# Causal attention with FFN on one core: masked quarters of the diagonal score blocks left out, short rows flipped, planner offsets split by token tile

## The chip, the cores and the metric

The kernel runs on one core of a Trainium2 chip. The metric is the device time of one execution in microseconds (us), lower is better.

## The reference, cut to what matters

The input is x of shape (8, 1024, 256): 8 batches of 1,024 tokens with 256 channels. All arithmetic is float32. There are 16 heads of width 64.

```
h   = layernorm(x)
q,k,v = h @ Wq, h @ Wk, h @ Wv                      # per head, 256 -> 64
s   = q k^T / 8 + rel_table[clip(j - i + 16, 0, 32)]   # bias by distance
s   = -inf where j > i                              # causal
a   = softmax(s) v ; o = concat(a) @ Wp + bp
x   = x + layernorm(o)
y   = layernorm(x); y' = y shifted by one token
r   = sigmoid((mu_r y + (1-mu_r) y') @ W_r)
f   = r * (relu((mu_k y + (1-mu_k) y') @ W_k)^2 @ W_v)
out = x + layernorm(f)
```

Only keys at or before the query count, so of each 128x128 block of scores on the diagonal the upper right triangle is masked. One quarter of that block, 64 queries by 64 keys, is masked in full.

## The kernel before

**Tiling.** The work is cut into 64 units, one for each batch and pair of heads. A unit's 1,024 queries are eight token tiles `tb` of 128 rows. Tile `tb` needs keys 0 to n = (tb + 1) x 128. Tiles 4 to 7 are "long" (n over 512): their scores are made in two parts of n/2 columns, each in one of two long PSUM tiles (`sl`, two banks each, both heads beside each other). Tiles 0 to 3 are "short": one part, with each head's scores in one of four single PSUM banks (`pm`). A unit is worked through in four steps, each with one long and one short tile: `STEPS = ((7, 1), (6, 0), (5, 3), (4, 2))`.

**Score matmuls (line 1000).** `part` in `do_scores` issues four matmuls: two output halves of 64 queries (`o` = 0 and 64, PSUM partitions 0 to 63 and 64 to 127) times two heads (64 rows of the array each). They use the array as four 64x64 tiles. All other matmuls contract over 128 rows and are issued in pairs of 64 output columns by the helper `matmul` (line 392), or likewise in `do_av` (line 1252), so the array is two 128x64 tiles there. The planner calls the two uses modes "rows" and "cols".

**Softmax.** For a part that reaches the diagonal, VectorE adds the bias with the mask from the table `bm` to the last 144 columns (`bias`, line 1029), then takes the negated row maximum (`top`, line 1037). ScalarE computes exp with the sum (line 1057). VectorE takes reciprocals (line 1124), GpSimd scales the rows (line 1145). The weights `p` are then transposed in 32x32 blocks by VectorE into `blocks` (line 1166), and 16 DMAs for each half unit (`shuffle`, line 1226) move the blocks into `d`, which `do_av` multiplies with v. Its result goes to `oT` (128 channels by 256 tokens), the stationary operand of `project_out`.

**Order.** Nothing is issued as it is written. `Planner.add` collects tasks, each with an engine, an assumed cost, buffers and a priority. `Planner.run` simulates the engines from these costs, and the instructions are then issued in the order of the best plan. A task's first priority is its step plus an offset from the table `RANK`, found by `kind(eng, fn)`, an engine and function name. `URGENT` is what a switch between the modes "rows" and "cols" costs in the choice of the next matmul task. Each engine carries out its queue in order, SP's DMA queue too.

**Start.** A prologue loads weights, builds one row of the bias table (`line`), writes it to DRAM as `skew`, and reads it back as `bm` with a row step that shifts each row by one column. Behind `bm` come the loads of `wp_sb` and of three raw FFN weights.

Of the kernel before, what the change touches and what calls it, by code (L numbers as in the profile page):

```python
# [8 lines left out]
F32 = mybir.dt.float32  # L9
# [30 lines left out]
SWITCH = 0.09  # L40
ISSUE = 0.66
STEP = 9.0
URGENT = 1.05


RANK = {
    "pe:part.go": -0.82,
    "dve:top.go": 1.9,
    "act:exp.go": -3.14,
    "dve:bias.go": 1.02,  # L50
    "pool:do_scores.behind": 6.53,
    "act:do_scores.<lambda>": -2.87,
    "pool:do_scores.both": 6.86,
    "dve:do_scores.<lambda>": -0.11,
    "pool:do_scores.<lambda>": -4.38,
    "pool:scale.go": 6.48,
    "dve:one.go": 1.8,
    "pe:do_qk.go": -0.33,
    "act:do_qk.<lambda>": -20.88,
    "sp:shuffle.move": 21.5,  # L60
    "pe:do_v.go": 0.57,
    "act:do_v.<lambda>": 11.6,
    "sp:load_wqk.go": -9.79,
    "sp:load_wv.go": 1.65,
    "pe:do_av.go": 0.22,
    "act:save.<lambda>": -6.41,
    "sp:load_rows.<lambda>": -6.4,
    "dve:norm_stats.go": 2.38,
    "pe:one.go": -0.19,
    "dve:one.plus_old": -14.51,  # L70
    "pool:normed.power": -0.11,
    "pool:normed.go": 6.49,
    "dve:by_dma.<lambda>": -1.51,
    "sp:by_dma.leave": -24.02,
    "sp:by_dma.<lambda>": -17.77,
    "act:by_dma.place": 4.69,
    "pool:plus.go": -26.3,
    "pool:s2.<lambda>": -47.14,
    "act:s3.go": 2.12,
    "dve:s4.go": 3.56,  # L80
    "pe:s5.go": 0.53,
    "act:s5.<lambda>": 17.56,
    "pool:s5.<lambda>": -0.97,
    "pe:second.go": -2.43,
    "act:s6.<lambda>": 22.56,
    "dve:s7.<lambda>": -5.69,
    "sp:s9.<lambda>": -14.9,
    "pe:some.go": 1.42,
    "act:normed.go_edge": -15,
}  # L90


def kind(eng, fn):
    return eng + ":" + ".".join(x for x in fn.__qualname__.split(".")[-3:] if x != "<locals>")


class Buf:
# [10 lines left out]
class Ring:  # L108


    def __init__(self, pool, shape, tag, n):
        self.pool, self.shape, self.tag, self.n, self.owners = pool, shape, tag, n, []

    def __call__(self, name, view=None):
        return Buf(self, name, view)
# [2 lines left out]
class Task:  # L118


    def __init__(self, eng, cost, fn, prio, mode, banks, mb):
        self.eng, self.cost, self.fn, self.prio, self.mode = eng, cost, fn, prio, mode
        self.banks, self.held, self.readers, self.mb = banks, (), [0] * banks, mb
        self.deps, self.after, self.makes, self.frees = [], [], [], []
        self.users, self.behind, self.left, self.first, self.seen = [], [], 0, 0.0, None


class Planner:
# [5 lines left out]
    ENGINES = ("pe", "sp", "act", "dve", "pool")  # L134

    def __init__(self, banks):
        self.tasks, self.gate = [], None
        self.free = dict.fromkeys(self.ENGINES, 0.0)
        self.mode, self.moved = None, 0.0
        self.bank_free = dict.fromkeys(range(banks), 0.0)  # L140

    def add(
# [12 lines left out]
    ):  # L155


        t = Task(eng, cost, fn, prio, mode, banks, mb)
        t.deps = list(deps)
        if self.gate is not None:  # L160
            t.deps.append(self.gate)
# [116 lines left out]
    def run(self, rounds, urgent=1.0, rank={}):  # L278

        new, self.tasks = self.tasks, []  # L280
        for t in new:
            deps = {}
            for d in t.deps:
                deps.update(dict.fromkeys(d if isinstance(d, list) else [d]))
            deps.pop(t, None)
            for d in deps:
                if d.seen is None:
                    d.users.append(t)
                    t.left += 1
                else:  # L290
                    t.first = max(t.first, d.seen)
            for d in dict.fromkeys(t.after):
                if d is not t and d not in deps and d.seen is None:
                    d.behind.append(t)
                    t.left += 1
        best, prio = None, {t: (t.prio + rank.get(kind(t.eng, t.fn), 0.0)) * STEP for t in new}
        for _ in range(rounds):
            plan = self.simulate(new, prio, urgent)
            if best is None or plan[0][-1][2] < best[0][-1][2]:
                best = plan  # L300
            prio = self.late(*plan[:2])
        order, held, state = best
        self.free, self.bank_free, self.mode, self.moved = state
        for t, _, _, seen in order:
            t.held = held.get(t, ())
            for b in t.makes:
                b.tile = b.ring.pool.tile(
                    b.ring.shape, F32, tag=b.ring.tag, name=b.name, bufs=b.ring.n
                )
                if b.view is not None:  # L310
                    b.tile = b.view(b.tile)
            t.fn()
            t.seen = seen
# [3 lines left out]
def tile_attn_ffn_block(  # L317
# [57 lines left out]
    acts = ctx.enter_context(tc.tile_pool(name="acts", bufs=1))  # L375

    bank = [ps_m.tile([P, HB], F32, name=f"pm{i}") for i in range(4)]
    plan = Planner(len(bank))
    add = plan.add

    def pm(t, i=0):

        return bank[t.held[i]]
# [4 lines left out]
    def matmul(dst, lhs, rhs, first, last):  # L388
# [18 lines left out]
        "ynT": Ring(acts, [P, NC, CT + 1], "ynT", 1),  # L407
        "q": Ring(acts, [P, T], "q", 2),
        "k": Ring(acts, [P, T], "k", 2),
        "v": Ring(acts, [P, NT, P], "v", 1),  # L410
        "sl": Ring(ps_l, [P, 2, HB], "sl", 2),
        ("p", "long"): Ring(acts, [P, T], "pl", 3),
        ("p", "short"): Ring(acts, [P, HB], "ph", 4),
        "carry": Ring(small, [P, NC], "carry", 2),
# [30 lines left out]
    def load_wqk(u, prio):  # L445

        pr = units[u][1]
        for name, w in (("q", Wq), ("k", Wk)):
# [9 lines left out]
                    )  # L458

            add("sp", 2 * ISSUE, go, w=[buf], prio=prio)  # L460

    def load_wv(u, prio):
        pr = units[u][1]
# [187 lines left out]
    def project_out(b, c, prs, prio):  # L651
# [6 lines left out]
        def one(k):  # L658
            def go():
                for pr in prs:  # L660
                    matmul(
                        pm(t)[:, :C],
                        oT[b, pr, c].tile[:, (1 - k) * P : (2 - k) * P],
                        wp_sb[:, pr, :],
                        (pr == prs[0]),
                        (pr == prs[-1]),
                    )

            t = add(
                "pe",  # L670
# [303 lines left out]
    def do_scores(u, tb, prio):  # L974


        n = (tb + 1) * P
        size = "long" if n > HB else "short"
        parts = [(0, n // 2), (n // 2, n)] if n > HB else [(0, n)]
        pr = units[u][1]  # L980
        q, k = qkv[u, "q"], qkv[u, "k"]
# [5 lines left out]
        def part(i, c0, c1):  # L987

            sl = R["sl"](f"s_{what}_{i}") if size == "long" else None
            keep = [sl] if sl else []  # L990

            def s(hh):
                return sl.tile[:, hh, : c1 - c0] if sl else pm(t, hh)[:, : c1 - c0]

            def go():
                for half in range(2):
                    for hh in range(2):
                        rows = slice(hh * D, (hh + 1) * D)
                        o = half * D
                        nc.tensor.matmul(  # L1000
                            s(hh)[o : o + D],
                            q.tile[rows, tb * P + o : tb * P + o + D],
                            k.tile[rows, c0:c1],
                            start=True,
                            stop=True,
                        )

            t = add(
                "pe",
                0.05 + (c1 - c0) * 0.00169,  # L1010
                go,
                r=[(q, tb // 4)] + [(k, g) for g in range((c1 - 1) // HB + 1)],
                w=keep,
# [8 lines left out]
            def bias(h0, h1):  # L1022
                def go():
# [1 line left out]
                        dst = sl.tile[:, :, c1 - c0 - w : c1 - c0]  # L1025
                        src = bm[:, 2 * pr : 2 * pr + 2, BW - w :]
                    else:
                        dst, src = s(h0)[:, n - w : n], bm[:, 2 * pr + h0, BW - w :]
                    nc.vector.tensor_tensor(dst, dst, src, ALU.add)  # L1029

                cost = 0.07 + (h1 - h0) * w / 960
                done = add("dve", cost, go, t, bm_done, r=keep, prio=prio - 0.5)
                ready.update({hh: done for hh in range(h0, h1)})

            def top(h0, h1):
# [115 lines left out]

        for hh in range(2):
            scale(hh)
        return z

    def turn(z, prio):

# [6 lines left out]
        def one(hh, p):  # L1164
# [9 lines left out]
                add("dve", 0.065 + n / 960, go, *state["move"], r=[p], prio=prio)  # L1174
            )

        for hh in range(2):
            one(hh, z["p"][hh])

    def turn_by_pe(z, g, prio):  # L1180

# [119 lines left out]
    with tc.tile_pool(name="prep", bufs=1) as prep:  # L1301
# [36 lines left out]
            prio=-4,  # L1338
        )
        bm_done = add("sp", ISSUE, lambda: nc.sync.dma_start(bm, moved), skew_done, prio=-4)  # L1340
        load_wv(0, -3)
        wp_done = add(
            "sp",
# [16 lines left out]
        for g in range(2):  # L1360
            do_qk(0, "k", g, -2)
            do_qk(0, "q", g, -2)
        load_wqk(1, -1)
        for half in range(2):
            soft[0, half] = do_scores(0, STEPS[0][half], -1)
        add(
# [62 lines left out]
    for m in range(LAST):  # L1429
# [3 lines left out]
            for half in range(2):  # L1433
                soft[m + 1, half] = do_scores(nu, STEPS[nst][half], m)
        if st == 0:
            do_av(u - 1, 0, m)
        if st == 2:
            do_av(u - 1, 1, m)
            do_v(u, 0, m + 0.3)
        if st == 3:  # L1440
            if u + 2 < NU:
                load_wqk(u + 2, m)
            do_v(u, 1, m + 0.3)
            if u + 1 < NU:
                load_wv(u + 1, m)
        if m + 1 < LAST:
# [7 lines left out]
            else:  # L1454
                turn(soft.pop((m, half)), m)
        if st % 2 and (u < NU - 1 or st == 1):
            shuffle(u, st // 2, m)
        if st == 0:
            do_qk(u + 1, "k", 0, m + 0.4)
            do_qk(u + 1, "k", 1, m + 0.6)  # L1460
        elif st == 1:
            do_qk(u + 1, "q", 1, m + 0.4)
        elif st == 2:
            do_qk(u + 1, "q", 0, m + 0.4)
    b = B - 1
    for g in range(2):
        do_av(NU - 1, g, LAST)
# [46 lines left out]
```

## Time and profile before

| | |
|---|---|
| time, median of 3 runs | 2208.03 us (2206.36 to 2208.11) |
| the profiled execution's own time | 2206.46 us |
| its span, first to last instruction | 2204.7 us, granted TensorE clock 0.997 |
| TensorE (PE) busy | 2172.5 us (99%) |
| VectorE (DVE) busy | 1967.5 us (89%) |
| GpSimd (POOL), ScalarE (ACT) busy | 1524.2 us (69%), 1412.6 us (64%) |
| DMA | 388.92 MB in 272,596 packets; the main queue holds 72.1% of 16 engines |

"Busy" is the time in which the engine has at least one instruction under way. The chain of work that ended last gives 92% of the span to PE. PE matmuls are pipelined and their ends are modelled, so it is best to read starts: the time from one group's start to the next group's start.

### The profile page before, as it was taken

The page shows a single profiled execution, that of the slowest core. Times are in us where ns is not written, and L with a number is a line of the kernel's source. Part 1 is how long each engine was busy: PE and PEld are TensorE (multiplying, and loading weights), DVE is VectorE, ACT ScalarE, POOL GpSimd, SP SyncE. Part 2 cuts the span into 40 slices and gives each one's busy share as a digit, 9 for nine tenths or more (in the row PEclk, how much of TensorE's full clock was granted, in tenths as well). Part 3 has the DMA queues.
Part 4 walks back from the last instruction along what each step waited for, and adds up shares of the span by engine and source line. Part 5 has one row for each costly group of instructions (what it writes and reads, how often), then busy time and mean ns, then how long its engine had stood idle before and what let it go on. Part 6 is the DMA issues. An engine that isn't in the chain of part 4 may idle for free.

```text
span 2204.7 us, 61232 instructions
## 1 busy us (share of the span) xinstructions
PE 2172.5 (99%) x21312; PEld 1175.2 (53%) x21312; DVE 1967.5 (89%) x4460; ACT 1412.6 (64%) x4314; POOL 1524.2 (69%) x3709
## 2 busy tenths in 40 slices
PE   7999999999999999999999999999999999999997
PEld 3455555555555545555555555555555555555565
DVE  5989999989999899998999889999898989999876
ACT  5666766657576676766667566666666656666554
POOL 4666677766777667776677757776677866677553
PEclk9999999999999999999999999999999999999999
DMA  5878877778777887777877787777777768777560
GB/s 159 188 179 204 197 176 173 173 192 194 184 168 174 195 192 173 173 172 194 190 177 173 168 205 191 176 173 170 196 186 174 180 167 214 180 183 180 128 160 25
DMA packets 272596, 388.92 MB, mean 176 GB/s; under 512 B 142624, under 2 KB 199968, under 8 KB 272160
## 3 DMA queue, kind: packets, MB, share of 16 engines
q1 hardware_dynamic: 272144, 384.87, 72.1%
q8 instruction: 170, 2.79, 0.5%
q14 instruction: 138, 1.13, 0.2%
q10 hardware_dynamic: 144, 0.14, 0.0%
HBM read 59.91 MB, written 25.29 MB: 39 GB/s over the span
## 4 chain that ended last, share of the span: by engine, by line
PE 92%; DVE 4%; DMA 1%; POOL 1%; ACT 1%; issue 0%; SPq 0%; ACTq 0%; DVEq 0%; POOLq 0%
PE pm L392 47%; PE pm L1252 22%; PE s L1000 16%; PE pm L1000 7%; DVE nmax L1037 1%; DVE blocks L1166 1%; DMA out_dram<-r 1%; DMA skew<-line 0%; DMA raw<-in_L_ffn_W_r_dram 0%; POOL p L1145 0%; ACT p L1057 0%; DVE pm L1029 0%; DVE xk L801 0%; DVE s L1029 0%; DMA tab<-in_L_attn_rel_table_dram 0%
## 5 line engine op out<-in xcount | busy, mean ns | idle before, releaser
L1145 POOL TENSOR_SCALAR p<-p,rcp 128x512 f32<-128x512 f32 (+5 forms) x1536 | 882.9, 591 | 108.7 <-DVE rcp L1124 77.1
L1057 ACT ACTIVATE p<-s,nmax 128x512 f32<-128x512 f32 (+3 forms) x1024 | 618.9, 607 | 416.2 <-DVE nmax L1037 320.2
L1166 DVE STREAM_TRANSPOSE blocks<-p 128x256 f32<-128x256 f32 (+1 forms) x1016 | 733.1, 754 | 46.1 <-POOL p L1145 38.3
L1037 DVE TENSOR_REDUCE nmax<-s 128x2 f32<-128x1024 f32 (+3 forms) x512 | 519.8, 1015 | 22.0 <-PE s L1000 18.1
L1252 PE MATMUL pm<-d,v 128*64 128x256 f32 (+1 forms) x5120 | 523.4, 359 | 0.0
L1252 PEld LDWEIGHTS pm<-d,v 128*64 128x64 f32 x5120 | 351.8, 137 | 217.9 <-issue 36.8
L1000 PE MATMUL s<-k,q 64*64 64x512 f32 (+3 forms) x4096 | 415.9, 517 | 5.6 <-ACT p L1057 5.4
L1057 ACT ACTIVATE p<-pm,nmax 128x256 f32<-128x256 f32 (+3 forms) x512 | 267.6, 525 | 144.2 <-DVE nmax L1037 104.1
L1000 PEld LDWEIGHTS s<-k,q 64*64 64x64 f32 x4096 | 142.4, 132 | 215.3 <-issue 98.4
L392 PE MATMUL pm<-wv,xnT 128*64 128x128 f32 x4096 | 248.0, 274 | 0.0
L392 PE MATMUL pm<-xnT,wq 128*64 128x512 f32 x1024 | 243.9, 597 | 2.6 <-ACT p L1057 2.6
L392 PEld LDWEIGHTS pm<-wv,xnT 128*64 128x64 f32 x4096 | 226.6, 137 | 36.6 <-ACT p L1057 14.1
L392 PE MATMUL pm<-xnT,wk 128*64 128x512 f32 x1024 | 245.2, 600 | 0.0
L392 PE MATMUL pm<-wp_sb,oT 128*64 128x256 f32 x2048 | 242.7, 383 | 0.7 <-ACT oT L1275 0.7
L1037 DVE TENSOR_REDUCE nmax<-pm 128x1 f32<-128x256 f32 (+3 forms) x512 | 235.0, 475 | 0.0
L1057 ACT ACTIVATION_READ_ACCUMULATOR p<-s,nmax 128x1 f32 x1024 | 203.3, 199 | 0.0
L392 PEld LDWEIGHTS pm<-wp_sb,oT 128*64 128x64 f32 x2048 | 139.7, 137 | 114.1 <-issue 40.3
L1029 DVE TENSOR_TENSOR pm<-pm,bm 128x144 f32<-128x144 f32 (+1 forms) x512 | 131.0, 301 | 72.1 <-PE pm L1000 69.7
L1000 PE MATMUL pm<-k,q 64*64 64x256 f32 (+3 forms) x2048 | 194.5, 450 | 0.4
L1114 POOL TENSOR_TENSOR tot<-tot,rcp 128x4 f32<-128x4 f32 x256 | 51.1, 200 | 161.6 <-ACT p L1057 97.4
L1133 POOL TENSOR_TENSOR rcp<-rcp,part 128x4 f32<-128x4 f32 x256 | 51.9, 203 | 131.5 <-DVE part L1124 110.9
L392 PEld LDWEIGHTS pm<-xnT,wq 128*64 128x64 f32 x1024 | 67.7, 136 | 119.0 <-issue 101.8
(103 smaller groups left out, 2231.9 us busy)
## 6 DMA issues: line engine op xcount, KB each, us to landing
d<-blocks SPq DMA_DIRECT2D x2032, 144.0 KB, 2.6
xin<-in_L_attn_x_dram SPq DMA_DIRECT2D x32, 256.0 KB, 2.9
wq<-in_L_attn_Wq_dram SPq DMA_DIRECT2D x128, 64.0 KB, 2.2
wk<-in_L_attn_Wk_dram SPq DMA_DIRECT2D x128, 64.0 KB, 2.3
wv<-in_L_attn_Wv_dram SPq DMA_DIRECT2D x64, 128.0 KB, 2.9
xre<-in_L_attn_x_dram SPq DMA_DIRECT2D x32, 256.0 KB, 2.9
out_dram<-r SPq DMA_DIRECT2D x32, 256.0 KB, 2.2
via_in<-st_in SPq DMA_DIRECT2D x112, 64.0 KB, 1.9
```

The source lines that it names most:

```text
L392: nc.tensor.matmul(dst[rows], lhs[:, rows], rhs, start=first, stop=last)
L1000: nc.tensor.matmul(s(hh)[o : o + D], q.tile[rows, tb * P + o : tb * P + o + D], k.tile[rows, c0:c1], start=True, stop=True,)
L1029: nc.vector.tensor_tensor(dst, dst, src, ALU.add)
L1037: nc.vector.tensor_reduce(nmax.tile[:, i, h0:h1], sl.tile[:, :, : c1 - c0] if sl else s(h0), AX.X, ALU.max, negate=True,)
L1057: nc.scalar.activation(ps[hh].tile[:, c0:c1], s(hh), AF.Exp, bias=nmax.tile[:, i, hh : hh + 1], scale=1.0, accum_out=tot.tile[:, i, hh : h ...
L1114: nc.gpsimd.tensor_tensor(tot.tile, tot.tile, rcp.tile, ALU.mult)
L1133: lambda: nc.gpsimd.tensor_tensor(rcp.tile, rcp.tile, inv.tile[:, 0:1, :].to_broadcast([P, 2, 2]), ALU.mult),
L1145: nc.gpsimd.tensor_scalar(p, p, rcp.tile[:, i, hh : hh + 1], 1.0, ALU.mult, ALU.mult)
L1166: nc.vector.transpose(blocks[g][:, :, s0 : s0 + 2 * tb + 1 : 2, hh, :].rearrange("p r a j -> p a r j"), p.tile[:, :n].rearrange("p (a r j) ...
L1252: nc.tensor.matmul(dst, v[:, jt, rows], src, start=(jt == 0), stop=(jt == 2 * k + 1),)
```

## The change

1. `do_scores` leaves the masked quarter out. In the part that reaches the diagonal, the 64 queries that come first in the token tile (`at == 0`) are multiplied with 64 columns fewer. The columns not written keep what stood in PSUM, and the bias table adds the mask of -1e30 to them.
2. For short tiles the two halves of 64 queries change places in PSUM (`flipped`), so the shortened matmuls write partitions 64 to 127 there and partitions 0 to 63 in long tiles. A flipped bias table is needed: `load_bf` reads it for each unit from `skew` by two DMAs into a ring of two buffers. `project_out` puts the rows back by picking the columns of `oT` the other way round.
3. The two long score tiles are fixed tiles (`longs`, `Ring(..., fixed)`), and these and the four banks are set to zero at the start by VectorE.
4. `kind` takes a task's note as well: the token tile for score and transpose tasks, the group for V, AV and shuffle, the kind and half for Q and K. `RANK` has 113 offsets instead of 43, all with new values. `URGENT` goes from 1.05 to 0.48, and the planner's cost of a diagonal score task falls by 32 columns' worth.

```diff
-URGENT = 1.05
+URGENT = 0.48
 RANK = {
-    "pe:part.go": -0.82,
-    "dve:top.go": 1.9,
-    "dve:bias.go": 1.02,
...
+    "pe:part.go:6": -0.64,
+    "dve:top.go:6": 2.78,
+    "dve:bias.go:6": -2.19,
...
+    "dve:bias.go:3": 2.37,
+    "dve:top.go:3": -9.34,
...
 class Ring:
-    def __init__(self, pool, shape, tag, n):
+    def __init__(self, pool, shape, tag, n, fixed=None):
...
             for b in t.makes:
-                b.tile = b.ring.pool.tile(
-                    b.ring.shape, F32, tag=b.ring.tag, name=b.name, bufs=b.ring.n
-                )
+                if b.ring.fixed:
+                    b.tile = b.ring.fixed[b.ring.owners.index(b) % b.ring.n]
+                else:
+                    b.tile = b.ring.pool.tile(
+                        b.ring.shape, F32, tag=b.ring.tag, name=b.name, bufs=b.ring.n
+                    )
...
+    longs = [ps_l.tile([P, 2, HB], F32, name=f"sl{i}") for i in range(2)]
+    for t in bank + longs:
+        nc.vector.memset(t, 0.0)
...
+    def load_bf(u, prio):
+
+        pr = units[u][1]
+        buf = bf[u] = R["bf"](f"bf_{u}")
+
+        def go():
+            for o in (0, D):
+                nc.sync.dma_start(
+                    buf.tile[D - o : P - o],
+                    bass.AP(
+                        tensor=skew.tensor,
+                        offset=skew.offset + 2 * pr * WL + P - 1 + o * (H * WL - 1),
+                        ap=[[H * WL - 1, D], [WL, 2], [1, BW]],
+                    ),
+                )
+
+        add("sp", 2 * ISSUE, go, skew_done, w=[buf], prio=prio, mb=0.15)
...
-                    matmul(
-                        pm(t)[:, :C],
-                        oT[b, pr, c].tile[:, (1 - k) * P : (2 - k) * P],
-                        wp_sb[:, pr, :],
-                        (pr == prs[0]),
-                        (pr == prs[-1]),
-                    )
+                    for o in (0, D):
+                        at = (1 - k) * P + (D - o if c < NCP // 2 else o)
+                        nc.tensor.matmul(
+                            pm(t)[o : o + D, :C],
+                            oT[b, pr, c].tile[:, at : at + D],
+                            wp_sb[:, pr, :],
+                            start=(pr == prs[0]),
+                            stop=(pr == prs[-1]),
+                        )
...
+        flipped = size == "short"
...
-                for half in range(2):
+                for o in (0, D):
+                    at = D - o if flipped else o
+                    end = c1 - D if c1 == n and at == 0 else c1
                     for hh in range(2):
                         rows = slice(hh * D, (hh + 1) * D)
-                        o = half * D
                         nc.tensor.matmul(
-                            s(hh)[o : o + D],
-                            q.tile[rows, tb * P + o : tb * P + o + D],
-                            k.tile[rows, c0:c1],
+                            s(hh)[o : o + D, : end - c0],
+                            q.tile[rows, tb * P + at : tb * P + at + D],
+                            k.tile[rows, c0:end],
...
-                0.05 + (c1 - c0) * 0.00169,
+                0.05 + (c1 - c0 - (D / 2 if c1 == n else 0)) * 0.00169,
...
-                        dst, src = s(h0)[:, n - w : n], bm[:, 2 * pr + h0, BW - w :]
+                        dst, src = s(h0)[:, n - w : n], bf[u].tile[:, h0, BW - w :]
...
+        load_bf(0, -3.5)
         load_wv(0, -3)
...
         load_wqk(1, -1)
+        load_bf(1, -0.5)
...
                 load_wqk(u + 2, m)
+                load_bf(u + 2, m)
```

## The prediction

> **What bounds the kernel now.** I read the page's busy times and slices first, then what PE waited for, then PE's order of time in one step.
>
> ```profile
> PE 2172.5 (99%) x21312; PEld 1175.2 (53%) x21312; DVE 1967.5 (89%) x4460; ACT 1412.6 (64%) x4314; POOL 1524.2 (69%) x3709
> ...
> PE   7999999999999999999999999999999999999997
> ...
> PEclk9999999999999999999999999999999999999999
> ```
>
> PE is full in every slice but the first and last, at full clock. All waits listed for PE add to 22.3 us; the longest:
>
> ```profile
> PE pm L392 <- ACT xin L515: 9.6, 2, 8.4
> PE s L1000 <- ACT p L1057: 5.4, 4, 4.3
> ...
> PE pm L392 <- DVE xk L801: 2.3, 1, 2.3
> PE pm L392 <- DMA raw<-in_L_ffn_W_r_dram: 1.3, 1, 1.3
> ```
>
> The first belongs to the start, the third to the tail. In between PE's own work is the bound, so PE time that goes shortens the span until another engine is late. Next in line is DVE. PE's timeline gives the prices (start, length, rows):
>
> ```profile
> 1003.04 0.66 PE L1000 MATMUL pm<-k,q 64*64 64x256 f32 x8
> 1003.52 1.90 PE L1000 MATMUL s<-k,q 64*64 64x512 f32 x16
> 1005.35 1.95 PE L392 MATMUL pm<-wp_sb,oT 128*64 128x256 f32 x16
> ...
> 1014.59 0.45 PE L1000 MATMUL pm<-k,q 64*64 64x128 f32 x8
> 1014.86 1.68 PE L1000 MATMUL s<-k,q 64*64 64x448 f32 x16
> ...
> 1020.09 1.09 PE L1000 MATMUL pm<-k,q 64*64 64x512 f32 x8
> 1021.00 1.47 PE L1000 MATMUL s<-k,q 64*64 64x384 f32 x16
> ```
>
> From start to start the 128-column task takes 0.27 us, 256 columns 0.48, 512 columns 0.91: 0.64 us for 384 columns, 1.667 ns a column. Each call leaves two rows (two passes), and the eight rows of a task fit into that only four at a time: the four 64x64 tiles run beside each other. What stays at 128 columns is 0.27 - 0.21 = 0.06 us on the first pass after cols mode. Behind the 512 task, 1005.35 - 1003.52 = 1.83 us against 1.71 of columns: 0.12 us. So a visit to rows mode costs 0.18 us beside its columns.
>
> **The change part by part.**
>
> *Masked quarters.* Each of the 512 diagonal score tasks loses 64 columns in two of its four tiles, both in one column half: partitions 0 to 63 in long tasks, 64 to 127 in short ones. A half alone gains 64 x 1.667 ns = 0.107 us, but the task's other half takes as long as before. Whether time is gained depends on whether the ready half may go on. If both halves run free, all is gained: 512 x 0.107 / 2 = 27.3 us. If the halves must meet at each change of mode, what counts is the longer half of each visit. I took the visits from the built program's order: 328 before (294,912 columns), 326 after. Of these 132 hold a short task and then a long pair, 28 a long pair and then a short one, 20 a short one between the two long parts, all evened out; about 50 a short one alone, 51 a long pair alone, 20 the second long part alone, 20 a short one with only the first long part: there the shorter half just waits. The longer halves add to 283,136 columns: 11,776 x 1.667 ns = 19.6 us gained.
>
> Two rules of the Trainium skill bear on this. The trace's four rows start at 1003.042, .048, .055 and .062, and the second passes at 1003.308 to .328, while in the compiled program the two passes of one call follow each other. So the second call's first pass overtook the first call's second pass: the array's tiles do not wait for program order. "TensorE: Matmul & The Clock Gate", Part 3, "The mechanism", says the contrary: matmuls start and end strictly in program order. By that rule half 64 could never lead, only catch up, and only the 31 visits with a shortened long part before a short task would gain: 31 x 0.107 = 3.3 us. I go by the rows. "TensorEngine Tiling (Array Packing)", "Key Properties", says that tiles work independently but a change of tiling mode drains the engine. The 0.12 us behind the last pass fits a drain, but both halves end together everywhere in this trace, so no row shows whether one waits for the other. I take the drain: **-19.6 us**, and keep -27.3 as the far end.
>
> *Changes of mode.* 657 become 653, two visits fewer: 2 x 0.18 = **-0.4 us**. `URGENT` is lower, yet the built order has no more of them.
>
> *The start.* Six memsets stand at the head of DVE. No DVE memset is in the trace; the nearest row, a maximum over 128x512 of PSUM, took 0.68 us, so about 0.6 to 0.7 a bank or 5 us in all. DVE's first operation starts at 4.88 us, so 0 to 1 us is uncovered. On SP, four `bf` loads stand before `wp_sb` and the three raw weights; two issues of `wq` took 0.99 us there, so 2 us. PE already waits for the first raw weight:
>
> ```profile
> 25.10 1.09 PE L392 MATMUL pm<-ident,raw 128*64 128x128 f32 x16 [1.28 <-DMA raw<-in_L_ffn_W_r_dram]
> ```
>
> With nothing to cover it, the lateness adds here: **+2.5 us** (1 to 4). The first bias, at 23.93 us, is covered: `bm` was issued at 14.26 and takes 6.3 us, `bf` follows 1 us later.
>
> *`bf` loads later.* 128 issues of 0.59 us (2,737 issues held SP's queue 1,619 us) add 76 us to a queue with some 500 us free. 16,384 packets at 93 ns (72.1% of 16 engines over 272,144 packets) add 96 us of each DMA engine: 72 becomes 76%. In the built order 61 loads stand between the two shuffles of unit u - 2, and what they wait for, that unit's last short bias, comes before the second shuffle's own transposes. So nothing is held up: 0 (0 to 3 us).
>
> *VectorE's order.* No operation is added, but the new offsets put `top` straight behind its own `bias`. In the built order 98 such pairs become 679. The trace holds both kinds:
>
> ```profile
> 28.71 0.45 DVE L1029 TENSOR_TENSOR s<-s,bm 128x288 f32<-128x288 f32 x1
> 29.19 1.23 DVE L1037 TENSOR_REDUCE nmax<-s 128x2 f32<-128x1024 f32 x1
> ...
> 1032.43 0.46 DVE L1029 TENSOR_TENSOR s<-s,bm 128x288 f32<-128x288 f32 x1
> 1032.80 0.55 DVE L1037 TENSOR_REDUCE nmax<-pm 128x1 f32<-128x384 f32 x1
> ```
>
> A maximum over what was just written starts 0.03 us after the bias's end; one over another tile 0.09 us before it. Each pair costs 0.12 us: 581 x 0.125 = 73 us of DVE time. The skill's "VectorE: DVE Perf Modes", "The DRAIN you can't avoid", says the flush comes after every operation and chaining without a wait saves nothing, which would make this order free; the rows disagree, and I use them. DVE's load by units of a batch ran from 29.5 to 32.6 us:
>
> ```profile
> 902.40:936.00 33.60, 33.60 (x336) 17.96 (x334) 32.60 (x77) 23.35 (x70) 27.72 (x65) 1.00 0.77 183
> 936.00:969.60 33.60, 33.60 (x320) 17.18 (x316) 30.56 (x72) 22.13 (x67) 25.38 (x57) 1.00 0.78 185
> 969.60:1003.20 33.60, 33.60 (x344) 19.82 (x344) 29.51 (x69) 19.16 (x61) 23.26 (x57) 1.00 0.64 153
> ```
>
> (third figure: DVE). Each unit gets 73 / 64 = 1.14 us more, while PE's unit shrinks by 0.31 to 33.3. Only the heaviest unit of a batch goes over, by about 0.4 us: 8 x 0.4 = **+3 us**. The far end is that all 73 us show; the near end below nothing: two long tiles' maxima now come at once behind their bias in 208 cases against 98, so they are handed back earlier, and up to 5 us of PE's short waits may go.
>
> *Fixed tiles, `project_out`.* The same matmuls in the same number: 21,312 rows in both programs. 0.
>
> **Sum:** -19.6 - 0.4 + 2.5 + 3 = -14.5 us on the profiled execution's 2206.5: 2192. That execution lies 1.6 us under the median of the runs shown, so 2208.0 - 14.5 = **2193.5 us**.
>
> **The rivals.**
>
> A (0.47) is the sum above.
>
> B, the halves do not meet at a change of mode: -27.3 in place of -19.6, 2186 us (0.17). For it: tiles overtake. Against: the 0.12 us behind each visit.
>
> C, the halves keep step or program order: gain 0 to 3.3 us, so 2210 to 2213 (0.10). This is also the case that the change does nothing. Against: the overtaking above.
>
> D, DVE becomes the bound, which ends slower (0.16). Its place is the maximum that lets ScalarE free a score tile or bank; PE's weight loads already stand there:
>
> ```profile
> L1000 PEld LDWEIGHTS s<-k,q 64*64 64x64 f32 x4096 | 142.4, 132 | 215.3 <-issue 98.4 <-ACT p L1057 77.4 <-PE pm L1000 4.3
> ```
>
> The price is the 73 us. DVE is idle 237 us, but most of that is waiting for PE or GpSimd and cannot be moved at will. Without the 3 us, 17.5 us are gained; if more than 17.5 / 73 = 24% of the price reaches PE, the kernel is slower. At half it is 2208 + 19 = 2227.
>
> E, the offsets by tile also take out short waits in front of score tasks (0.10): 5 to 10 us under A, 2184 to 2188.
>
> **How the numbers follow.** About 0.2% (4.4 us) is what this measurement tells from no change. Faster by more: nearly all of A, B, E: 0.71. Within it: most of C and the edges of A and D: 0.11. Slower: D and the rest of C: 0.18. The range goes from B with a little of E, 2180, to 2212, over C's lower part and the mild part of D; the rest of D and something below stay out. Between them A gives 2193.
>
> **What would show it.** Right: rows-mode starts, in visits with short and long tasks together, come 0.107 us closer; PE's busy time falls by some 15 to 20 us and its waits stay under 35. B: starts after visits with a single task come closer as well. C: start-to-start times of score tasks unchanged. D: PE waits for ACT p or DVE of several tens of us, DVE over 95% between start and tail. The raw weights' wait at the start should be about 4 us. The prediction is wrong if the time is over 2204, or if PE's waits grow by more than 15 us.

## The result, and the profile after

The change makes the kernel slower: **2218.26 us** (median of 4 runs, 2216.15 to 2221.31) against 2208.07 us beside it (2206.36 to 2209.05), a ratio of 1.0048 with a 95% interval of 1.0035 to 1.0060. The forecast was 2193.5 us, 25 us lower, with its range ending at 2212. The profiled execution has a span of 2217.8 us at a granted TensorE clock of 0.996 (0.997 before), so the clock is not what changed.

The page of the changed kernel (lines are those of its own file: the score matmuls are L1110, `bias` L1139, `top` L1147, exp L1167):

```profile
PE 2169.2 (98%) x21312; PEld 1198.3 (54%) x21312; DVE 2026.9 (91%) x4466; ACT 1425.0 (64%) x4314; POOL 1523.7 (69%) x3709
...
DVE  5999999989999899998999999999999999999876
...
PE 68%; DVE 20%; DMA 4%; issue 3%; SPq 2%; POOL 1%; ACT 1%; DVEq 0%; ACTq 0%; POOLq 0%
```

PE is busy only 3.3 us less, at a span 13.1 us longer. VectorE has 59 us more, and the last line, the chain that ended last, now gives it 20% of the span, where it had 4%. What PE waited for (total, times, longest):

```profile
PE sl L1110 <- ACT p L1167: 15.1, 34, 3.7
PE pm L472 <- ACT xin L616: 9.6, 2, 8.4
PE pm L472 <- ACT p L1167: 5.9, 6, 2.7
PE pm L472 <- DMA raw<-in_L_ffn_W_r_dram: 2.6, 1, 2.6
PE pm L472 <- DVE xk L904: 2.3, 1, 2.3
```

Waits for a score tile that an exponential has to free went from 5.4 us in 4 places to 15.1 us in 34. The line of PE's weight loads for scores shows more of the same, 113.0 us behind an exponential where it was 77.4:

```profile
L1110 PEld LDWEIGHTS sl<-k,q 64*64 64x64 f32 x4096 | 161.0, 133 | 209.6 <-ACT p L1167 113.0
```

The eight units of one batch, by windows of a unit's length (figures: PE, PE loads, VectorE, ScalarE, GpSimd):

```profile
873.25:907.00 33.75, 33.29 (x300) 17.47 (x294) 32.26 (x74) 21.45 (x64) 25.26 (x60) 1.00 0.81 194
907.00:940.75 33.75, 33.41 (x314) 16.82 (x312) 31.39 (x73) 22.29 (x67) 25.40 (x60) 1.00 0.71 165
940.75:974.50 33.75, 33.46 (x366) 20.26 (x364) 33.05 (x75) 23.23 (x71) 26.77 (x62) 1.00 0.76 187
974.50:1008.25 33.75, 33.36 (x311) 18.20 (x308) 30.32 (x68) 19.88 (x60) 23.40 (x52) 1.00 0.77 186
1008.25:1042.00 33.75, 33.75 (x336) 18.81 (x334) 29.63 (x68) 20.57 (x65) 21.10 (x55) 1.00 0.70 173
1042.00:1075.75 33.75, 33.75 (x348) 18.33 (x346) 32.45 (x66) 24.51 (x78) 21.97 (x60) 1.00 0.87 206
1075.75:1109.50 33.75, 33.63 (x346) 18.55 (x346) 31.76 (x69) 23.63 (x72) 22.85 (x61) 1.00 0.81 195
1109.50:1143.25 33.75, 33.75 (x344) 18.51 (x336) 31.44 (x74) 20.58 (x62) 26.84 (x63) 1.00 0.73 176
```

PE is no longer full in five of these eight windows. VectorE fits into each of them, with 33.05 of 33.75 us in the worst, and PE still loses time where VectorE has 30.3 or 31.4. So the loss is not load over capacity; it is lateness at the moment when a tile is wanted. A piece of the chain shows one case:

```profile
920.81 0.85 DVE nmax L1147
921.66 0.38 DVE sl L1139
922.05 0.02 issue
922.07 0.96 DVE nmax L1147
923.03 0.07 DVE rcp L1234
923.10 1.02 DVE blocks L1287
924.12 0.02 issue
924.14 0.68 ACT p L1167 x2
924.82 0.04 issue
924.87 0.48 PE sl L1110
```

VectorE works without a pause: a maximum, a bias, 0.02 us, the maximum over the same tile, a reciprocal, a transpose. The exponential waits for that transpose, which stood in VectorE's queue behind the maxima, and PE waits for the exponential (ScalarE's and PE's timelines; in brackets the idle time before):

```profile
924.14 0.58 ACT L1167 ACTIVATE p<-sl,nmax 128x384 f32<-128x384 f32 x1 [0.35 <-DVE blocks L1287]
...
923.73 0.86 PE L1110 MATMUL pm<-k,q 64*64 64x384 f32 x8
924.87 1.33 PE L1110 MATMUL sl<-k,q 64*64 64x320 f32 x16 [0.28 <-ACT p L1167]
```

Start to start this short task takes 1.14 us; 384 columns were priced at 0.64, with 0.06 at the head of a visit. PE's 0.28 us in brackets is only what lies behind the modelled end, so PE's listed waits understate the loss. I therefore counted stalls from starts. For each visit to rows mode and each stretch of cols mode, I took the time from its first start to the next one's and subtracted its columns (1.667 ns each on the longer half; 1/1.2 ns in cols mode). Where more than 0.27 us stays, I count what is over 0.18. From 40 to 2100 us that gives 10.4 us in the kernel before and **42.1 us** in the changed one, 31.7 us more.

The shortened products themselves are as forecast:

```profile
1021.67 0.44 PE L1110 MATMUL pm<-k,q 64*64 64x128 f32 x8
1021.85 1.67 PE L1110 MATMUL sl<-k,q 64*64 64x448 f32 x16
1023.45 1.97 PE L472 MATMUL pm<-wv,xnT 128*64 128x128 f32 x32
...
1027.06 1.08 PE L1110 MATMUL pm<-k,q 64*64 64x512 f32 x8
1027.88 0.90 PE L1110 MATMUL sl<-k,q 64*64 64x384 f32 x8
```

The task of 512 columns is followed after 0.82 us where it was 0.91, and the visit with 128 and twice 448 columns takes 1.78 us.

And the pairs of bias and maximum cost VectorE what was forecast:

```profile
1002.69 0.31 DVE L1139 TENSOR_TENSOR pm<-pm,bf 128x144 f32<-128x144 f32 x1
1003.04 0.56 DVE L1147 TENSOR_REDUCE nmax<-pm 128x1 f32<-128x384 f32 x1
1003.51 0.31 DVE L1139 TENSOR_TENSOR pm<-pm,bf 128x144 f32<-128x144 f32 x1
1003.85 0.56 DVE L1147 TENSOR_REDUCE nmax<-pm 128x1 f32<-128x384 f32 x1
```

The maximum over what the bias has just written starts 0.03 to 0.04 us after the bias's end. The next bias, in another bank, starts 0.09 us before the maximum's end.

### The profile page after: what moved, and what is told of

It is laid out like the page before. It is cut to its first block, busy times and chain, and to the rows that moved or that the text cites. A ratio compares the mean times of both kernels' runs of the same rounds, so it can differ in the third digit from the quotient of the medians.

```text
span 2217.8 us, 61424 instructions
## 1 busy us (share of the span) xinstructions
PE 2169.2 (98%) x21312; PEld 1198.3 (54%) x21312; DVE 2026.9 (91%) x4466; ACT 1425.0 (64%) x4314; POOL 1523.7 (69%) x3709
## 3 DMA queue, kind: packets, MB, share of 16 engines
q1 hardware_dynamic: 290576, 394.31, 73.9%
## 4 chain that ended last, share of the span: by engine, by line
PE 68%; DVE 20%; DMA 4%; issue 3%; SPq 2%; POOL 1%; ACT 1%; DVEq 0%; ACTq 0%; POOLq 0%
PE pm L472 27%; PE pm L1375 15%; PE sl L1110 13%; PE pm L764 8%; DVE blocks L1287 7%; DVE nmax L1147 6%; PE pm L1110 5%; SPq L1349 2%; DVE xr L904 1%; DVE sl L1139 1%; DMA d<-blocks 1%; DVE pm L1139 1%; ACT p L1167 1%; DVE xk L904 1%; POOL p L1255 1%
## 5 line engine op out<-in xcount | busy, mean ns | idle before, releaser
L1167 ACT ACTIVATE p<-sl,nmax 128x512 f32<-128x512 f32 (+3 forms) x1024 | 617.6, 606 | 406.3 <-DVE nmax L1147 278.7
L1287 DVE STREAM_TRANSPOSE blocks<-p 128x256 f32<-128x256 f32 (+1 forms) x1016 | 723.2, 750 | 58.2 <-POOL p L1255 50.1
L1147 DVE TENSOR_REDUCE nmax<-sl 128x2 f32<-128x1024 f32 (+3 forms) x512 | 519.6, 1015 | 20.0 <-PE sl L1110 12.6
L1110 PE MATMUL sl<-k,q 64*64 64x384 f32 (+4 forms) x4096 | 422.0, 507 | 15.7 <-ACT p L1167 15.1
L1167 ACT ACTIVATE p<-pm,nmax 128x256 f32<-128x256 f32 (+3 forms) x512 | 269.8, 528 | 220.7 <-DVE nmax L1147 154.6
L1110 PEld LDWEIGHTS sl<-k,q 64*64 64x64 f32 x4096 | 161.0, 133 | 209.6 <-ACT p L1167 113.0
L1147 DVE TENSOR_REDUCE nmax<-pm 128x1 f32<-128x256 f32 (+3 forms) x512 | 250.6, 490 | 16.2
L472 PEld LDWEIGHTS pm<-wv,xnT 128*64 128x64 f32 x4096 | 225.0, 137 | 39.9 <-issue 19.6
L1167 ACT ACTIVATION_READ_ACCUMULATOR p<-sl,nmax 128x1 f32 x1024 | 201.0, 196 | 0.0
L1110 PE MATMUL pm<-k,q 64*64 64x448 f32 (+7 forms) x2048 | 191.2, 423 | 0.0
L1139 DVE TENSOR_TENSOR pm<-pm,bf 128x144 f32<-128x144 f32 (+1 forms) x512 | 151.5, 296 | 37.9 <-PE pm L1110 36.1
```

Of the source, the lines that this page charges most:

```text
L472: nc.tensor.matmul(dst[rows], lhs[:, rows], rhs, start=first, stop=last)
L1110: nc.tensor.matmul(s(hh)[o : o + D, : end - c0], q.tile[rows, tb * P + at : tb * P + at + D], k.tile[rows, c0:end], start=True, stop=True,)
L1147: nc.vector.tensor_reduce(nmax.tile[:, i, h0:h1], sl.tile[:, :, : c1 - c0] if sl else s(h0), AX.X, ALU.max, negate=True,)
L1167: nc.scalar.activation(ps[hh].tile[:, c0:c1], s(hh), AF.Exp, bias=nmax.tile[:, i, hh : hh + 1], scale=1.0, accum_out=tot.tile[:, i, hh : h ...
L1287: nc.vector.transpose(blocks[g][:, :, s0 : s0 + 2 * tb + 1 : 2, hh, :].rearrange("p r a j -> p a r j"), p.tile[:, :n].rearrange("p (a r j) ...
```

## The experiments

Each result is given with its ratio to the kernel before, timed beside it, and a 95% interval. The kernel before took 2207.5 to 2208.9 us in these sessions, so a difference between two sessions is uncertain by about 1.4 us. The theories: **P**, the pairs on VectorE; **O**, the new order as such; **F**, the fixed tiles, the `bf` loads and the start. "Pairs" is the number of maxima that stand directly behind their own bias (679 in the changed kernel, 98 before).

### Which order goes with which work (e1, e2)

Two crossings. The first keeps the new work and takes `RANK`, `URGENT` and `kind` back:

```diff
-URGENT = 0.48
+URGENT = 1.05
...
-    return ":".join([t.eng, ".".join(path), t.note])
+    return ":".join([t.eng, ".".join(path)])
```

> The changed kernel with the offsets of before (43 kinds, URGENT 1.05); masked quarters, flip, bias loads, fixed tiles and zeroing stay. Its built order has 727 changes of mode in place of 657 (35 visits more, 35 x 0.18 = +6 us), longer halves of 284,864 columns (-16.8 us) and 126 bias-then-maximum pairs on VectorE in place of 679. Theory P (the pairs on VectorE ate the gain): 2208 - 17 + 6 + 2.5 = about 2200 us. Theory O (the new order as such, not the pairs): about 2200 us as well. Theory F (fixed tiles, bias loads and the start ate it): 2215 us or more.

The second does the reverse: the new offsets, notes and `URGENT` with the old work.

> The kernel before with the new offsets, notes and URGENT alone: full columns, no flip, no bias loads, no fixed tiles. Its built order has 701 changes of mode (22 visits more, +4 us) and 694 pairs on VectorE. P and O: 2208 + 4 + the 28 us that the changed kernel lost against its sum without the VectorE term (2218 against 2190.5), about 2240 us. F: 2212 us.

Measured: **2226.55 us** (1.0076, 1.0063 to 1.0088) and **2297.86 us** (1.0405, 1.0391 to 1.0419). e1 misses P and O by 26 us and lies in F's "2215 us or more"; e2 misses every expectation. A set of offsets fits only the work that it was made with, so neither crossing isolates anything, and e1 is no evidence for F either: its order of PE is another.

Much of both can be accounted for all the same. The median visit takes 0.176 us over its columns, and the median cols stretch behind it 0.201, together 0.377 (medians of the kernel before). That is the most that a visit costs, since part of the 0.201 belongs to the stretch's own length: the median is 0.170 for stretches under 2 us. Against the kernel before, e2 has 22 visits more, up to 8.3 us, and 92.7 us of stalls where that had 10.4: 90.6 us, of 89 measured. e1 has 35 visits more, up to 13 us, 24 us more stalls, about 4 us for loads and start (below), less 17 us of columns: about 24 us, of 18 measured, so some 6 us stay open. And e1 has its 34.6 us of stalls with only 126 pairs. So stalls do not need pairs: an order can be late in other ways, and O is not nothing in general. From here on I left PE's order as it was in every experiment.

### The short pairs taken apart, PE's order unchanged (e3)

```diff
+def unpaired(order):
...
+    dve = [e for e in order if e[0].eng == "dve"]
+    for x, y, z in zip(dve, dve[1:], dve[2:]):
+        b0, m0, b1 = x[0], y[0], z[0]
+        if not (is_a(b0, "bias") and is_a(m0, "top") and is_a(b1, "bias")):
+            continue
+        if b0 in m0.deps and b0.deps[0] is b1.deps[0]:
+            order.remove(z)
+            order.insert(order.index(y), z)
+    return order
...
+        order = unpaired(order)
```

> The changed kernel in the same order, but where VectorE had bias 0, maximum 0, bias 1 of one short task, both biases now come first. 295 of the 679 pairs go (295 x 0.125 = 37 us of VectorE); PE's order is untouched. P: the loss of 28 us for 581 added pairs falls in proportion, -14 us, about 2204 us. O and F: 2218 us, within 3.

Measured: **2207.17 us** (0.9994, 0.9985 to 1.0003), 11.1 us under the changed kernel for 295 pairs taken apart, where P expected 14 and O and F expected none within 3. P holds; 0.038 us of the 0.125 of each pair reached the end.

### The other way round: pairs put into the kernel before (e5)

Each short bias of the kernel before is moved to stand directly ahead of its own maximum, 519 pairs more. PE's order stays.

```diff
+        for b in [d for d in m.deps if not isinstance(d, list) and is_a(d, "bias") and d in place]:
+            order.remove(place[b])
+            order.insert(order.index(e), place[b])
```

> The kernel before, with the bias of each short task moved back on VectorE to stand right ahead of its own maximum; no maximum moves and PE's order is that of before. The pairs go from 98 to 617. P (pairs cost PE time): at the 11.1 us that 295 pairs were worth in e3, 0.038 us each, 519 x 0.038 = +20 us, about 2228 us. O and F (the pairs matter only in the changed kernel's order, or not at all): 2209 us, within 4.

Measured: **2218.62 us** (1.0046, 1.0034 to 1.0059). The pairs alone, with none of the rest of the change, cost 10.9 us, about as much as the whole change loses. The price per pair is 0.021 us, half of what I expected. Stalls rose from 10.4 to 20.9 us, which accounts for it.

### Fixed tiles and loads (e6, e7)

The first keeps four of the 128 `bf` loads and leaves out 124 (the expectation says 126), with the two `bf` tiles fixed. The short tiles of all later units then add the bias of the first two units' heads; that is the part of the computation that is changed.

```diff
+    bfs = [ins.tile([P, 2, BW], F32, name=f"bf{i}") for i in range(2)]
...
-        "bf": Ring(ins, [P, 2, BW], "bf", 2),
+        "bf": Ring(ins, [P, 2, BW], "bf", 2, bfs),
...
-            for o in (0, D):
+            for o in (0, D) if u < 2 else ():
```

> The changed kernel in the same order, with 126 of the 128 flipped-bias loads... that is all but those of units 0 and 1, left out: short tiles of later units take the bias of the first two pairs of heads, so that part of the computation is another. SP keeps its order otherwise. F (the loads crowd SP's queue and the DMA engines): 2213 us or less. P and O: 2218 us, within 3.

The second gives the kernel before the fixed, zeroed score tiles.

> The kernel before with fixed long score tiles and the six memsets at the start, nothing else; all queues keep their order. F (fixed tiles bring waits): 2213 us or more. P and O: 2208 us plus at most 1 us for the memsets.

Measured: **2216.18 us** (1.0036, 1.0022 to 1.0050), about 2 us under the changed kernel, with intervals that overlap, and **2207.80 us** (0.9999, 0.9990 to 1.0008), no difference from the kernel before. So the fixed tiles cost nothing and the loads some 2 us at most; neither gives the 25 us by which the forecast missed.

### More pairs taken apart (e8, e10)

e8 puts both biases of every short task together and moves a long bias ahead of a reciprocal that stands before it; 191 pairs stay. e10 moves every long bias one place ahead where the plan has its scores ready; 102 stay.

```diff
+        if is_a(e[0], "bias"):
+            b0 = first.setdefault(e[0].deps[0], e)
+            if b0 is not e:
+                order.remove(e)
+                order.insert(order.index(b0) + 1, e)
```

> The changed kernel in the same PE order, with the second bias of every short task right behind the first, and a long bias ahead of a reciprocal where it stood behind it: 191 pairs are left of 679 (61 us of VectorE gone). P: 488 x 0.038 = -18.5 us against the changed kernel, about 2200 us, faster than both kernels. O: no better than e3, 2207 us.

> e8, and the bias of a long tile is moved one place ahead on VectorE wherever the plan has its scores ready by then; no maximum changes its place among the maxima. 102 pairs are left (98 before the change). P: 89 pairs x 0.038 = -3.4 us against e8, about 2196.5 us. If the moved biases wait for PE and hold up what stood ahead of them: 2200 us or more.

Measured: **2199.90 us** (0.9963, 0.9951 to 0.9976) and **2196.81 us** (0.9941, 0.9928 to 0.9955), 18.4 and 21.5 us under the changed kernel. Both expectations of P came in. VectorE's share of the chain that ended last, 20% in the changed kernel, is 6% in both. VectorE's timeline of e8 shows the move:

```profile
990.33 0.53 DVE L1164 TENSOR_TENSOR pm<-pm,bf 128x144 f32<-128x144 f32 x2
990.76 1.01 DVE L1172 TENSOR_REDUCE nmax<-pm 128x1 f32<-128x384 f32 x2
991.74 0.42 DVE L809 TENSOR_TENSOR y<-pm,bp_bc 128x256 f32<-128x256 f32 x1
```

Two biases and two maxima take 1.41 us from the first start to what follows; in the changed kernel the same four took 1.64 (1002.69 to 1004.33).

### What the quarters are worth (e4, e9)

Both write every score product over its full columns: e4 in the changed kernel, e9 in e8.

```diff
-                    end = c1 - D if c1 == n and at == 0 else c1
+                    end = c1
```

> The changed kernel in the same order with nothing left out of the score matmuls (end = c1 always). PE gets back 11,776 columns of the longer halves, 19.6 us. If the lost time is a constant of the start or the loads (F), or PE's waits stay as they are: 2218 + 20 = 2238 us. If VectorE has become the bound (P), the longer matmuls fill waits that PE has anyway: 2218 to 2226 us. O lies between, towards 2238.

> e8 with nothing left out of the score matmuls, same order. In the changed kernel's own order the masked quarters were worth 11.4 us (e4 against it). P says that the rest of their 19.6 us fell into waits for VectorE; with VectorE relieved they should be worth nearly all of it: 2199.9 + 19 = about 2219 us. If the 11.4 us is all that the quarters can give (the halves gain less than the visits say): 2211 us.

Measured: **2229.64 us** (1.0097, 1.0082 to 1.0113) and **2208.47 us** (1.0002, 0.9993 to 1.0011). So the quarters are worth 11.4 us in the changed kernel and, with most pairs gone, 8.6 us. My sum had 19.6. For e4, P expected at most 2226, and O a time between that and 2238; it came out at 2229.6. For e9, P's expectation that the rest would come back with the pairs gone (2219) is refuted.

The same four kernels show that pairs and quarters add. Taking 488 pairs apart is worth 21.2 us with full columns (e4 against e9) and 18.4 us with the quarters left out. A 3 us difference of such differences is hardly more than their scatter.

### VectorE relieved further (e13, e14)

What turns the other 11 us into waits: VectorE as a whole, or ScalarE's exponentials and the two long tiles as such? Both kernels build on e10 and let the long maxima read half their columns, so half of those comparisons are left out of the computation; e14 has full score columns besides.

```diff
-                        sl.tile[:, :, : c1 - c0] if sl else s(h0),
+                        sl.tile[:, :, (c1 - c0) // 2 : c1 - c0] if sl else s(h0),
                         AX.X,
```

> The kernel with the biases moved (102 pairs left), and VectorE relieved of a further part of its work: each maximum over a long score tile reads only the second half of its columns. What it takes out of the computation is half of those comparisons. By the rows of the trace it frees some 240 us of VectorE's 1983 us (512 maxima, 518 us, at a little under half). TensorE's instructions and their order are as they were. If VectorE is what turned the rest of the quarters' gain into waits, the 21 us of stalls inside the steady part of TensorE mostly go: about 2180 us. If it is ScalarE's exponentials or the two score tiles as such, the time stays within 5 us of 2196.8: 2192 or more.

> The same relieved kernel with every score product over its full columns (nothing left out). It is to be read against the relieved kernel before it. If VectorE is what kept the quarters from being worth the 19 us of the sum, they are worth 16 to 19 us now: about 2197 us. If something else keeps it, the distance stays at 8 to 11 us, as it was with VectorE loaded: about 9 us over the relieved kernel, whatever that one gives.

Measured: **2184.14 us** (0.9892, 0.9878 to 0.9906) and **2203.02 us** (0.9974, 0.9965 to 0.9983). The quarters are now worth **18.9 us**. Both came out above their expected times, e13 4 us over its 2180 and e14 6 us over its 2197: of some 21 us of stalls 11 stayed. But the difference of the two, on which the question hung, is the upper end of what was expected of VectorE and far from the 8 to 11 of the other theory. e13's page:

```profile
PE 2151.4 (99%) x21312; PEld 1215.5 (56%) x21312; DVE 1796.2 (82%) x4466; ACT 1398.8 (64%) x4314; POOL 1521.8 (70%) x3709
...
PE 96%; DVE 1%; DMA 1%; SPq 1%; ACT 0%; POOL 0%; issue 0%; ACTq 0%; POOLq 0%; DVEq 0%
```

VectorE is down by 187 us against e10 (240 expected) while ScalarE (1411.8 there) and GpSimd (1523.0) are nearly as they were, and the chain is PE's again. The shorter maxima also release their own tiles sooner (0.69 us for 512 of 1,024 columns, where all took 1.22), so the runs do not separate VectorE's load from the length of a single maximum; either way it is VectorE. PE's largest wait in the steady part is

```profile
PE sl L1137 <- ACT p L1194: 3.4, 2, 2.9
```

Stalls, counted as above in the profiled executions, nearly close the account:

| left out / full columns | stalls | quarters worth | worth plus added stalls |
|---|---|---|---|
| changed kernel / e4 | 42.1 / 32.8 us | 11.4 us | 20.7 us |
| e8 / e9 | 24.7 / 13.1 us | 8.6 us | 20.2 us |
| e13 / e14 | 11.2 / 8.3 us | 18.9 us | 21.8 us |

In each row, what the quarters are worth and what comes back as stalls add to 20 to 22 us; 19.6 had been priced.

### The start, and the best version (e11, e12)

e11 is e8 with the second `bf` load of the start (two of its four DMAs) moved behind the raw FFN weights on SP; e12 adds that to e10.

```diff
+        order.remove(bfs[1])
+        order.insert(order.index(ffn[0]) + 1, bfs[1])
```

> e8 with the second flipped-bias load of the start moved behind the raw FFN weights on SP. PE's wait for the first raw weight, 2.4 us in e8 and 1.3 us before the change, should fall by about 1 us: about 2199 us. If the start's lateness lies elsewhere: 2200 us, no difference.

> The two gains found so far in one kernel: every movable bias off its own maximum (2196.8 us alone) and the second mask load of the start behind the raw FFN weights (about 1.3 us less when it was added to the lesser move). If they add, 2195.5 us; if the start's gain is swallowed by a later wait, 2196.8 us or more.

Measured: **2198.55 us** (0.9949, 0.9935 to 0.9962) and **2193.65 us** (0.9935, 0.9921 to 0.9949). The medians are 1.4 us under e8 and 3.2 us under e10, but the runs of each pair overlap (e11 2192.27 to 2198.63, e8 2198.42 to 2201.34; e12 2193.51 to 2197.02, e10 2193.64 to 2197.92), so a gain from the load's place is likely and not shown. e12 beats both kernels: 14.7 us under the one before and 24.6 under the changed one.

## Why the prediction was wrong

**The VectorE term is the step that failed.** The prediction had 581 pairs, 0.125 us each, 73 us of VectorE time; the pairs and their price came out as said. Then it went on: "Only the heaviest unit of a batch goes over, by about 0.4 us", +3 us. That compared sums by unit, as if VectorE's work could slide within 33.6 us. The windows of the changed kernel contradict it: five of eight units lose PE time, and none has VectorE over its capacity. What counted is the delay of single operations of VectorE in front of two long tiles and four banks. PE's listed waits for exponentials from 40 to 2100 us, followed back to ScalarE's last idle time, ended at a maximum in 11.2 of 20.1 us, at reciprocals and transposes in the rest. The runs put the pairs' price at 18.4 us for 488 pairs and 21.5 for 577 (e8, e10), in reverse 10.9 for 519 in the kernel before (e5).

**The quarters' term was right as PE work and wrong as time.** 19.6 us became 11.4 (e4) and 8.6 (e9), because a PE that is faster asks for its tiles sooner of a VectorE that is no faster: stalls rose by 9.3 and 11.6 us. With VectorE relieved they gave 18.9. Adding the two terms was not the error, since e4 and e9 show that they add within 3 us. The first was weighed against VectorE's idle time in a unit and the second against no other engine; neither was weighed against what waits for VectorE.

**Ledger** from measured medians (each step is a difference of two runs, so it must close; what it tells is the size of the steps): kernel before 2208.1; the new order, loads, start and fixed tiles with full columns and 191 pairs, +0.4 (e9); quarters -8.6 (e8); 488 pairs back, +18.4: 2218.3. Against the sum: pairs 15 us too low, quarters 11 too high, and some 2 given back by the rest.

**Rival D named the mechanism** and gave 24% of the pairs' price as its point of decision. 18.4 us of 488 x 0.125 = 61 us is 30%. So D's sum with 30% of all 73 us gives a loss of some 4 us; the rest of the measured 10 came from the quarters, which D had left at their full worth. It had the place right too (the maximum before the exponential that frees a tile, and the weight loads' wait). Its own sign, "DVE over 95% between start and tail", did not come: VectorE's share from 40 to 2100 us is 93.6% (1927 of 2060 us). The sign was too strict for a queue that must be on time. The general sign came: PE's listed waits grew by 15.4 us, from 22.3 to 37.7.

**A against B and C.** Halves of unequal length may lead within a visit. Visits of a short task and then a long pair keep an overhead of 0.18 us over their longer half (median; 0.176 before, with equal halves), so each gained its 0.107 us. Tasks that stand alone gained next to nothing: a lone short one takes 0.153 us over its longer half against 0.166, a lone long pair 0.171 in both kernels. So the halves meet at the change of mode, as the Trainium skill's "TensorEngine Tiling (Array Packing)", "Key Properties", has it. B and C are out, and the strict order that the skill's "TensorE: Matmul & The Clock Gate", Part 3, "The mechanism", states does not hold between these tiles.

**Small terms.** Changes of mode: a visit costs up to 0.377 us, not 0.18, since the cols stretch behind it pays as well; for two visits that is nothing, for e1 it was up to 13 us. The start: PE's first V group came at 41.26 us in the changed kernel's profile where it was 37.43, but at 38.16 in e3, 38.59 in e4 and 39.88 in e8, which load the same at the start. So the lateness is 0.7 to 3.8 us with 2.5 forecast, and one profile can't fix it; the raw weights' wait was 2.6 us, not the 4 forecast. `bf` loads: some 2 us, inside the 0 to 3 given; the DMA queue stands at 73.9% for 76 forecast. Fixed tiles: 0, right. E: e9 should take 2208.1 + about 4 for loads and start + 93 added pairs at 0.02 to 0.04, about 2215, and took 2208.5; so the new order may be some 6 us better apart from its pairs. That is worked out, and no run shows it by itself.

## What to carry to other kernels

When the engine at the bound gets faster and the next one sits at 90%, do not test the next one's sum by stage; ask which of its operations are waited for, and price the delay of those. A price on such an engine can't be put at nothing because its idle time is larger: here about 30% of the added VectorE time, spread in steps of 0.125 us, reached the end (17% when the pairs were put into the kernel before), and about half of the first engine's own gain was handed back as well. Look for a place where the order of two neighbours costs time: an independent operation between a write and its reader gave 18 to 21 us without touching a matmul.

## What the runs showed of the hardware

In the changed kernel a maximum starts 34 ns after the end of the bias whose output it reads (median of 679; each waits on a semaphore that the bias raises). The operation behind it, which does not read its result, starts 83 ns before the maximum's end, and in the kernel before a maximum behind the bias of another tile starts 91 ns before that one's end (medians). All of these biases and maxima read PSUM. The Trainium skill's "VectorE: DVE Perf Modes", "The DRAIN you can't avoid", says that chaining cannot skip the flush, and adds that a next operation that is not held starts earlier. The prediction read the first part alone; the rows fit the second, and e3 and e8 show what hiding the flush by the order alone was worth.

Not expected was how PE's visits react to the tiles. A visit with halves of unequal length runs on without a gap where a short and a long task complement each other. And time beside the columns is spent on both sides of a change of tiling: 0.176 us in the rows visit and 0.201 in the cols stretch behind it (medians of the kernel before; 0.170 for cols stretches under 2 us).
